# A decoder layer with a mixture of experts: the shared expert's products moved and stripped of their ones-products, b2 added as a row, the end divided among three engines

## The chip, the cores and the metric

The kernel runs on one core of a Trainium2 chip. Its engines work side by side, each through its own list of instructions in order: TensorE (PE in the profile, with PEld for its weight loads), VectorE (DVE), ScalarE (ACT), GpSimd (POOL) and SyncE (SP, which here only issues DMAs). ACT and POOL can issue DMAs too. Engines wait for one another by semaphores. The metric is the device time of one execution in microseconds (us); lower is better.

## The reference, cut to what matters

Two sequences of 1024 tokens with 256 features (N = 2048 tokens) go through self-attention, cross-attention over 77 context tokens, and a feed-forward block with 8 experts of which each token uses two. Each block sees a normalized input and is added to the running `x`. The change touches the end of cross-attention and the feed-forward block:

```python
probs = softmax(flat @ gate_W)                       # 2048 x 8
topk_w, topk_idx = top_k(probs, 2)
topk_w = topk_w / topk_w.sum(-1, keepdims=True)
combine = (one_hot(topk_idx, 8) * topk_w[..., None]).sum(1)
out = 0.5 * gelu(flat @ shared_W + shared_b)         # the shared expert
for e in range(8):
    h = gelu(flat @ W1[e] + b1[e])                   # 256 -> 1024
    out = out + combine[:, e:e+1] * (h @ W2[e] + b2[e])   # 1024 -> 256
out = layernorm(out, eps=1e-5) * gamma + beta
x = x + out
```

## The kernel before

All is float32. A *token tile* is 128 tokens (16 of them); a *chunk* c is four token tiles (4 chunks). `xs` holds x for all tokens, `xnT` the normalized input with features on the partitions, `acc` the feed-forward result of all tokens.

**Self-attention** takes the first 560 us and is not touched.

**Cross-attention and the sort.** One loop (before's lines 962 to 986) writes PE's order out by hand; the other engines' order is made by a scheduler from the same program. Per token tile i, `scores(i)` makes the products with the keys on PE, then DVE adds a mask and takes the maximum (L888), POOL subtracts it (L889), ACT takes the exponential (L892), DVE sums (L894) and inverts, POOL multiplies (L896); `turn(i)` transposes the result on PE into PSUM tiles named ppT, and ACT copies them. Per chunk, `queries(c)` prepares; `attend(c)` multiplies by the values in two halves (`pco`, L921, eight matmuls each, ACT copying each half into `oT`), then projects (`pu`, L933), and DVE adds the result to `xs` (L941); `gate(c)` normalizes `xs`, writes the rows to a DRAM table `xnd`, transposes them on PE into `xnT`, multiplies by the gate (`pg`, L953) and calls `choose(c)`: some 17 small DVE operations that find each token's two experts, `taken`, and the running count `earlier` (L764).

The sort turns this into a list of rows for each expert. `place(c)` multiplies `taken` and `earlier` by triangular and full matrices of ones on PE (`prk`, L772 and L776), then DVE computes each pair's slot and two one-hot tiles `row` and `col` (L802), and ACT multiplies `row` by the pair's number (L810). `invert(c)` multiplies `col` and `row` on PE (`pin`, L820) and DVE adds it into `places`. After chunk 3 the counts `pcn` give the tiles' owners; `ppk` (L1045), a product of `places`, gives `to_row` and `from_row` (L1053).

`shared(c)` is the shared expert: for each of the chunk's four token tiles a product of a row of ones with the bias row `fsb` (L833, the ones-product), and two products of `xnT` with `fsw` (L837), summed in PSUM; ACT takes Gelu of 128x1024 values into `acc` (L844). In PE's order shared(0) stands after place(2), shared(1) before place(3), shared(2) between place(3) and invert(3), and shared(3) after the sort, before the experts. POOL adds `beta_f` to `xs` with `add_rows` (L190), chunk by chunk, where the scheduler puts it.

**Experts.** The sorted pairs fill tiles of 256 rows, each with one expert: at least 16 (FULL), at most 23, and 19 in this run's data. For tile i, `fetch(i)`, issued two tiles ahead, loads the owner's W1 and W2 (1 MB each, SP's queue, three buffers each) and gathers the tile's rows `xg` by two indirect DMAs on POOL's queue (three buffers). `first_layer(i)` transposes `xg` on PE (`px`, L1134), DVE copies it to `xgT`, PE makes the products `ph` (L1144), ACT takes Gelu with b1 into `hT` (L1151). `second_layer(i)` multiplies by W2 (`po`, L1161), DVE copies the result to `y` (L1168), and two indirect DMAs on POOL's queue scatter it to a DRAM table `pairs` (L1171). PE's order is first_layer(0), first_layer(1), second_layer(0), first_layer(2), second_layer(1), and so on, with the transposes drawn a little ahead.

**End.** `weigh` made the two weights of each token and `comb`, tokens by experts. `biases(c)` transposes `comb`, multiplies by `b2` on PE (`pb2`, L1100), and DVE writes acc = 0.5 acc + pb2 (L1101). Then for each chunk two loads `yt` from `pairs` (SP's queue, four buffers), eight DVE operations that add weight x `yt` to `acc` (L1225), and `affine_residual`: DVE statistics (L149, L150), the power -0.5 on POOL (L142), and eight DVE operations (L197, L201) that normalize, scale by `gamma_f` and add `xs`; the chunk is stored from SP's queue.

Of the kernel before, what the change touches and what calls it, by code (L numbers as in the profile page):

```python
# [8 lines left out]
F32 = mybir.dt.float32  # L9
# [5 lines left out]
P = 128  # L15
# [23 lines left out]
def decoder_kernel(  # L39
# [73 lines left out]
    def load_bcast(src, name):  # L113
        t = const.tile([P, D], F32, name=name)
        nc.sync.dma_start(out=t, in_=src.rearrange("(o d) -> o d", o=1).to_broadcast([P, D]))
        return t
# [572 lines left out]
    fsb = rt.tile([1, D], F32, name="fsb")  # L689
    nc.sync.dma_start(out=fsb, in_=f_sb.rearrange("(o d) -> o d", o=1))  # L690
    b1 = rt.tile([E, HID], F32, name="b1")
    nc.scalar.dma_start(out=b1, in_=f_b1)
    b2 = rt.tile([E, D], F32, name="b2")
    nc.scalar.dma_start(out=b2, in_=f_b2)
# [133 lines left out]
    def shared(c):  # L828

        psh = big("psh").rearrange("p a (t f) -> p (a t) f", f=D)  # L830
        for t in range(4):
            tt = 4 * c + t
            nc.tensor.matmul(  # L833
                psh[:, t, :], lhsT=ones[0:1, :], rhs=fsb, start=True, stop=False
            )
            for kc in range(2):
                nc.tensor.matmul(  # L837
                    psh[:, t, :],
                    lhsT=xnT[:, kc, tt * P : (tt + 1) * P],
                    rhs=fsw[:, kc, :],  # L840
                    start=False,
                    stop=(kc == 1),
                )
        nc.scalar.activation(acc[:, 4 * c : 4 * c + 4, :], psh, AF.Gelu)  # L844

    with tc.tile_pool(name="cr1", bufs=1) as cr1, tc.tile_pool(name="cr2", bufs=2) as cr2:
# [65 lines left out]
        def attend(c):  # L912
            b = c // 2
            PT = PTs.pop(c)
            oT = cr2.tile([P, 2, 512], F32, tag="oT", name=f"oT{c}")
            for G in range(2):
                po = one("pco")
                for i in range(2):
                    for r in range(4):
                        h = 8 * G + 2 * r + i  # L920
                        nc.tensor.matmul(  # L921
                            po[32 * r : 32 * r + 32, :],
                            lhsT=vx[:T2, b, h, :, :].rearrange("p i d -> p (i d)"),
                            rhs=PT[:T2, h, :],
                            start=(i == 0),
                            stop=(i == 1),
                        )
                nc.scalar.copy(oT[:, G, :], po)
            for u in range(2):
                pu = one("pu").rearrange("p (t f) -> p t f", f=D)  # L930
                for t in range(2):
                    for G in range(2):
                        nc.tensor.matmul(  # L933
                            pu[:, t, :],
                            lhsT=oT[:, G, P * (2 * u + t) : P * (2 * u + t) + P],
                            rhs=cwu[:, G, :],
                            start=(G == 0),
                            stop=(G == 1),
                        )
                x2 = xs[:, 4 * c + 2 * u : 4 * c + 2 * u + 2, :]  # L940
                nc.vector.tensor_tensor(x2, x2, pu, ALU.add)  # L941
# [20 lines left out]
        with tc.manual_schedule(engines={nc.tensor.engine}):  # L962
            queries(0)
            for i in range(NT + 7):
                if i < NT:
                    scores(i)
                if 0 <= i - 2 < NT:
                    turn(i - 2)
                if i % 4 == 1 and i + 3 < NT:
                    queries(i // 4 + 1)  # L970
                if i % 4 == 3 and i > 3:
                    attend(i // 4 - 1)
                if i % 4 == 2 and i > 6:
# [12 lines left out]
            invert(3)  # L986
# [8 lines left out]
    with tc.tile_pool(name="ff1", bufs=1) as ff1, ExitStack() as later:  # L995
# [75 lines left out]
        shared(3)  # L1071
# [3 lines left out]
        comb = ff1.tile([P, NT, E], F32, name="comb")  # L1075

        def weigh():
# [6 lines left out]
            sel = ff1.tile([P, 2, NT, E], F32, name="selw")  # L1084
            nc.vector.tensor_tensor(
                sel, hots, wts.unsqueeze(3).to_broadcast([P, 2, NT, E]), ALU.mult
            )
            nc.vector.tensor_tensor(comb, sel[:, 0], sel[:, 1], ALU.add)

        def biases(c):  # L1090

            a4 = acc[:, 4 * c : 4 * c + 4, :]
            pct = one("pct").rearrange("p (t f) -> p t f", f=P)
            for t in range(4):
                nc.tensor.transpose(pct[:E, t, :], comb[:, 4 * c + t, :], ident)
            cT = ff1.tile([E, 4, P], F32, tag="cT", name="cT", bufs=2)
            nc.vector.tensor_copy(cT, pct[:E, :, :])  # L1097
            pb2 = big("pb2").rearrange("p a (t f) -> p (a t) f", f=D)
            for t in range(4):
                nc.tensor.matmul(pb2[:, t, :], lhsT=cT[:, t, :], rhs=b2, start=True, stop=True)  # L1100
            nc.vector.scalar_tensor_tensor(a4, a4, 0.5, pb2, ALU.mult, ALU.add)  # L1101
# [4 lines left out]
        hTs = [ff2.tile([P, NH, TS], F32, name=f"hT_{k}") for k in range(2)]  # L1106
        ys = [ff2.tile([P, 2, D], F32, name=f"y_{k}") for k in range(2)]

        def fetch(i):

            e = nc.sync.value_load(owner_i[0:1, i : i + 1], min_val=0, max_val=E - 1)
            w1, w2, xg = w1s[i % 3], w2s[i % 3], xgs[i % 3]
# [5 lines left out]
            )  # L1118
            for s in range(2):
                nc.gpsimd.indirect_dma_start(  # L1120
# [7 lines left out]
            return w1, w2, xg  # L1128

        def first_layer(i, w1, xg):  # L1130
# [8 lines left out]
            for q in range(2):  # L1139
                ph = big("ph").rearrange("p a (h f) -> p (a h) f", f=TS)  # L1140
                for j in range(4):
# [9 lines left out]
                    nc.scalar.activation(  # L1151
# [4 lines left out]
        def second_layer(i, w2, hT):  # L1156
# [11 lines left out]
            nc.vector.tensor_copy(y, po)  # L1168
# [44 lines left out]

        for c in range(4):
            biases(c)
        for c in range(4):
            a4 = acc[:, 4 * c : 4 * c + 4, :]
            for i in range(2):
                r0 = N * i + 512 * c
                yt = ff2.tile([P, 4, D], F32, tag="yt", name=f"yt_{c}{i}", bufs=4)  # L1220
                nc.sync.dma_start(
                    out=yt, in_=pairs[r0 : r0 + 512, :].rearrange("(t p) d -> p t d", p=P)
                )
                for t in range(4):
                    nc.vector.scalar_tensor_tensor(  # L1225
                        a4[:, t, :], yt[:, t, :], wts[:, i, 4 * c + t : 4 * c + t + 1],
                        a4[:, t, :], ALU.mult, ALU.add,
                    )
            affine_residual(a4, a4, c, gamma_f, 1e-5)
# [40 lines left out]
```

## Time and profile before

| What | Value |
|---|---|
| Time, three runs | 1150.11, 1150.76, 1152.16 us; median 1150.76 us |
| The profiled execution | 1148.25 us, span of its instructions 1146.4 us, mean granted PE clock 0.911 |
| Busy share of the span | PE 86%, PEld 49%, DVE 55%, ACT 44%, POOL 32% |
| choose(3) ended on DVE | 763.34 us |
| rows known (L1053) | 790.46 us |
| first transpose of the experts | 802.04 us |
| last matmul of the experts | 1087.7 us |
| first `yt` used | 1098.24 us |
| last DVE operation | 1140.95 us |
| weights (38 loads of 1024 KB, SP's queue) | median 8.7 us from issue to landing |
| gathers and scatters (38 each, POOL's queue) | median 6.2 and 3.0 us to landing |

How to read it: times within the kernel count from the span's start. A row of the timeline gives the start, the time that the group of instructions took, engine, line, operation, output <- inputs, shapes and count, and in brackets how long the engine sat idle before it and what ended that. A row of the waits gives who waited for whom: us in total, times, longest. A matmul of float32 appears as two passes. The granted clock is a share of PE's full clock.

### The profile page before, as it was taken

To read this page: it belongs to the slowest core of one execution; us is meant where nothing else is said; L and a number is where in the kernel's file an instruction comes from. 1 tells how busy PE (TensorE), PEld (TensorE's weight loads), DVE (VectorE), ACT (ScalarE), POOL (GpSimd) and SP (SyncE) were. 2 spreads that over 40 slices of the span, in tenths; PEclk is the share of its full clock that TensorE was granted. 3 is DMA by queue.
4 is the path that set the end of the run, shared out by engine and by line. 5 is a ranking of instruction groups with operands and counts; after the bars stand their busy time and mean duration, and the time that the engine had idled before them with its cause. 6 is when DMAs were issued, how large, how long until landed. Compare 5 with 4: busy or idle time off the path is not lost. (4 is left out here: it accounts for less than half of the span.)

```text
span 1146.4 us, 15580 instructions
## 1 busy us (share of the span) xinstructions
PE 984.9 (86%) x5926; PEld 563.2 (49%) x5926; DVE 627.1 (55%) x1208; ACT 502.3 (44%) x953; POOL 372.2 (32%) x308
## 2 busy tenths in 40 slices
PE   4889999999897999999367877899999999999940
PEld 2543333333332333332134555566888888887830
DVE  6776668778867788884785797442000000000167
ACT  1237667767664677779035343221322222222100
POOL 2123224443322333335576535113222222222101
PEclk9989999999898999999689887775999999999955
DMA  9100000000000000000000000005444445544042
GB/s 170 28 1 1 1 2 1 1 1 1 1 1 1 1 2 1 1 1 1 11 0 1 18 1 19 20 18 191 158 163 170 173 169 184 184 166 139 18 135 92
DMA packets 56741, 64.46 MB, mean 56 GB/s; under 512 B 17636, under 2 KB 49546, under 8 KB 56658
## 3 DMA queue, kind: packets, MB, share of 16 engines
q1 hardware_dynamic: 43634, 52.57, 13.6%
q0 software_dynamic: 3648, 9.18, 2.2%
q10 hardware_dynamic: 9376, 1.61, 1.0%
q8 instruction: 50, 0.82, 0.3%
q14 instruction: 33, 0.27, 0.1%
HBM read 54.97 MB, written 9.18 MB: 56 GB/s over the span
## 5 line engine op out<-in xcount | busy, mean ns | idle before, releaser
L516 DVE TENSOR_REDUCE mx<-sA 128x1 f32<-128x512 f32 x512 | 317.6, 683 | 87.6 <-PE sB L552 75.6
L560 ACT ACTIVATE pt<-sB 128x512 f32<-128x512 f32 x512 | 266.3, 611 | 113.7 <-PE sB L552 113.0
L509 PE MATMUL sA<-kT,qc 32*128 32x512 f32 x1024 | 264.6, 631 | 0.0
L552 PE MATMUL sB<-qB,kT 32*128 32x512 f32 x1024 | 253.0, 625 | 10.4 <-DVE mx L516 10.4
L582 POOL TENSOR_TENSOR avs<-avs,part 128x512 f32<-128x512 f32 x112 | 142.9, 1276 | 307.1 <-ACT part L581 306.7
L1151 ACT ACTIVATE hT<-ph,b1s 128x256 f32<-128x256 f32 x152 | 72.0, 474 | 200.0 <-PE ph L1144 200.0
L1168 DVE COPY y<-po 128x512 f32<-128x512 f32 x19 | 13.1, 692 | 259.8 <-PE po L1161 259.8
L509 PEld LDWEIGHTS sA<-kT,qc 32*128 32x128 f32 x1024 | 102.5, 187 | 91.2 <-ACT pt L560 56.1
L1161 PE MATMUL po<-w,hT 128*128 128x256 f32 x608 | 138.8, 382 | 5.6 <-DVE y L1168 5.6
L569 PE MATMUL av<-pt,vaug 128*32 128x512 f32 x1024 | 141.1, 612 | 0.9 <-ACT pt L560 0.9
L1144 PE MATMUL ph<-xgT,w 128*128 128x256 f32 x608 | 137.0, 384 | 0.5 <-DVE xgT L1138 0.5
L1161 PEld LDWEIGHTS po<-w,hT 128*128 128x128 f32 x608 | 114.1, 190 | 24.2 <-DVE y L1168 9.4
L552 PEld LDWEIGHTS sB<-qB,kT 32*128 32x128 f32 x1024 | 100.4, 187 | 51.0 <-issue 32.0
L1144 PEld LDWEIGHTS ph<-xgT,w 128*128 128x128 f32 x608 | 107.2, 190 | 27.4 <-ACT hT L1151 8.2
L1120 POOL DMA_INDIRECT xg<-xnd,from_row x38 | 37.1, 976 | 132.5 <-PE px L1134 88.9
L1171 POOL DMA_INDIRECT pairs<-y,to_row x38 | 38.3, 1007 | 125.9 <-DMA pairs<-y,to_row 76.2
L581 ACT COPY part<-av 128x512 f32<-128x512 f32 x112 | 69.0, 616 | 8.7 <-PE av L569 8.6
L569 PEld LDWEIGHTS av<-pt,vaug 128*32 128x32 f32 x1024 | 21.6, 109 | 101.3 <-DVE mx L516 84.2
L142 POOL TENSOR_TENSOR rstd<-rstd,nhalf 128x4 f32<-128x4 f32 x20 | 21.5, 1076 | 114.4 <-DVE rstd L141 114.0
L889 POOL TENSOR_TENSOR st<-st,cm 128x1232 f32<-128x1232 f32 x16 | 37.2, 2324 | 41.7 <-DVE cs L895 17.0
L908 ACT COPY PT<-ppT 77x1024 f32<-77x1024 f32 x32 | 30.8, 1005 | 43.7 <-PE ppT L907 43.7
L907 PE MATMUL ppT<-ident,st 128*77 128x128 f32 x256 | 37.5, 307 | 12.5 <-POOL st L896 6.8
(201 smaller groups left out, 998.9 us busy)
## 6 DMA issues: line engine op xcount, KB each, us to landing
w<-in_L_ffn_W_dram SPq DMA_DIRECT2D x38, 1024.0 KB, 8.7
yt<-pairs SPq DMA_DIRECT2D x8, 512.0 KB, 3.8
xs<-in_x_dram SPq DMA_DIRECT2D x4, 512.0 KB, 7.0
xnd<-xn SPq DMA_DIRECT2D x4, 512.0 KB, 2.9
out_dram<-acc SPq DMA_DIRECT2D x4, 512.0 KB, 3.0
mk<-in_mask_BxSxS_ik_dram SPq DMA_DIRECT2D x1, 616.0 KB, 4.6
xg<-xnd,from_row POOLq DMA_INDIRECT x38, 6.2
pairs<-y,to_row POOLq DMA_INDIRECT x38, 3.0
```

What stands on the lines that cost most here:

```text
L509: nc.tensor.matmul(s, lhsT=units[h // 4, "q"][r0 : r0 + 32, q0 : q0 + P], rhs=units[h // 4, "k", g % 2][r0 : r0 + 32, 512 * kh : 512 * kh ...
L516: nc.vector.tensor_reduce(largest[h][:, qt, hh : hh + 1, kh], s, AX.X, ALU.max)
L552: nc.tensor.matmul(s, lhsT=units[h // 4, "k", g % 2][r0 : r0 + 32, kt * P : (kt + 1) * P], rhs=shifted[h][r0 : r0 + 32, :], start=True, st ...
L560: nc.scalar.activation(powers[m, hh], s, AF.Exp, scale=1.0 / 16.0)
L569: nc.tensor.matmul(av[32 * hh : 32 * hh + 32, :], lhsT=vaug[:, kt, 4 * g + hh, :, b], rhs=powers.pop((m, hh)), start=True, stop=True,)
L581: nc.scalar.copy(part, av)
L582: nc.gpsimd.tensor_tensor(sums[h], sums[h], part, ALU.add)
L907: nc.tensor.transpose(pp[:T2, h, :], st[:, 8 * G + h, :], ident)
L1144: nc.tensor.matmul(ph[:, j, :], lhsT=w1[:, kc, hc * P : (hc + 1) * P], rhs=xgT[:, kc, :], start=(kc == 0), stop=(kc == 1),)
L1151: nc.scalar.activation(hT[:, hc, :], ph[:, j, :], AF.Gelu, bias=b1s[:, i, hc : hc + 1])
L1161: nc.tensor.matmul(po[:, s, :], lhsT=hT[:, hc, s * P : (s + 1) * P], rhs=w2[:, hc, :], start=(hc == 0), stop=(hc == NH - 1),)
L1171: nc.gpsimd.indirect_dma_start(out=pairs[:, :], out_offset=bass.IndirectOffsetOnAxis(ap=to_row[:, k : k + 1], axis=0), in_=y[:, s, :], in_ ...
```

## The change

- `shared(c)` has no ones-product any more; its two products per token tile start and stop the sum alone, and ACT copies the sum to `acc` without Gelu. `fsb` is loaded as a tile with the row on all partitions; POOL adds it to `acc` (128x1024, one operation a chunk), and after `hidden[1]` (the last Gelu of tile 1's hidden layer) `finish_shared(c)` takes Gelu of `acc` on ACT and halves it on DVE.
- PE's order around the sort: shared(0) stands between turn(14) and turn(15); place(c) stands between the two halves of attend(c+1); then attend(3) with place(2), shared(1), invert(2), gate(3), shared(2), place(3), pcn, shared(3), invert(3).
- POOL's `beta_f` additions, `fsb` additions and `weigh` are held behind the gathers of tiles 0 and 1. On POOL's list they now stand in this order: four gathers, the power of `weigh`, four fsb additions, four beta additions, then tile 2's gathers.
- `biases`, `comb` and b2's matmuls are gone. `fetch` loads the owner's b2 as a row on all 128 partitions (128 KB, SP's queue after W2, three buffers), and `y` is po + b2 on DVE instead of a copy.
- At the end the eight `yt` loads go into the weights' buffers, issued together from SP's and ACT's queues. Chunks 0 to 2: DVE adds the pairs and makes the statistics, ACT scales and shifts (four operations of 128x256), POOL multiplies by `gamma_f` and adds `xs` (two operations of 128x1024). Chunk 3 keeps `affine_residual` on DVE.

```diff
     def shared(c):
         psh = big("psh").rearrange("p a (t f) -> p (a t) f", f=D)
         for t in range(4):
             tt = 4 * c + t
-            nc.tensor.matmul(
-                psh[:, t, :], lhsT=ones[0:1, :], rhs=fsb, start=True, stop=False
-            )
             for kc in range(2):
                 nc.tensor.matmul(
                     psh[:, t, :],
                     lhsT=xnT[:, kc, tt * P : (tt + 1) * P],
                     rhs=fsw[:, kc, :],
-                    start=False,
+                    start=(kc == 0),
                     stop=(kc == 1),
                 )
-        nc.scalar.activation(acc[:, 4 * c : 4 * c + 4, :], psh, AF.Gelu)
+        nc.scalar.copy(acc[:, 4 * c : 4 * c + 4, :], psh)
...
                 nc.scalar.copy(oT[:, G, :], po)
+                if G == 0 and halfway is not None:
+                    halfway()
...
             queries(0)
-            for i in range(NT + 7):
+            for i in range(NT + 3):
...
                 if i % 4 == 3 and i > 3:
-                    attend(i // 4 - 1)
+                    attend(i // 4 - 1, (lambda c=i // 4 - 2: place(c)) if i > 7 else None)
+                if i == NT:
+                    shared(0)
                 if i % 4 == 2 and i > 6:
                     gate(i // 4 - 2)
-                if i % 4 == 3 and i > 10:
-                    place(i // 4 - 2)
-                if i == NT + 3:
-                    shared(0)
                 if i % 4 == 1 and i > 12:
                     invert(i // 4 - 3)
+            attend(3, halfway=lambda: place(2))
             shared(1)
+            invert(2)
+            gate(3)
+            shared(2)
             place(3)
             pcn = one("pcn")
             nc.tensor.matmul(pcn[:, :E], lhsT=ones, rhs=earlier[:, NT, :], start=True, stop=True)
-            shared(2)
+            shared(3)
             invert(3)
...
-        shared(3)
         sorting.__exit__(None, None, None)
...
-        def biases(c):
+        def finish_shared(c):
             a4 = acc[:, 4 * c : 4 * c + 4, :]
...
+            nc.scalar.activation(a4, a4, AF.Gelu)
+            nc.vector.tensor_scalar(a4, a4, 0.5, None, ALU.mult)
...
+            nc.sync.dma_start(out=b2, in_=f_b2[bass.ds(e, 1)].to_broadcast([P, D]))
             for s in range(2):
-                nc.gpsimd.indirect_dma_start(
+                fetched[i] = nc.gpsimd.indirect_dma_start(
...
-            nc.vector.tensor_copy(y, po)
+            nc.vector.tensor_tensor(y, po, b2.unsqueeze(1).to_broadcast([P, 2, D]), ALU.add)
...
         got = {0: fetch(0), 1: fetch(1)}
-        with tc.issue_after(sorted_at.ins):
+        with tc.issue_after(sorted_at.ins), tc.issue_after(fetched[1].ins):
             weigh()
-        for c in range(4):
-            add_rows(c, beta_f)
-        behind = tiles((0, FULL), FULL + 2, got, None)
+            for c in range(4):
+                a4 = acc[:, 4 * c : 4 * c + 4, :]
+                nc.gpsimd.tensor_tensor(
+                    a4, a4, fsb.unsqueeze(1).to_broadcast([P, 4, D]), ALU.add
+                )
+            for c in range(4):
+                add_rows(c, beta_f)
+        behind = tiles((0, 2), FULL + 2, got, None)
+        with tc.issue_after(hidden[1].ins):
+            for c in range(4):
+                finish_shared(c)
+        behind = tiles((2, FULL), FULL + 2, got, behind)
...
+        land = [w.rearrange("p a f -> p (a f)") for w in w1s + w2s]
+        yts = {}
         for c in range(4):
-            biases(c)
+            for i in range(2):
+                yt = land[c][:, 4 * D * i : 4 * D * (i + 1)].rearrange("p (t d) -> p t d", d=D)
+                r0 = N * i + 512 * c
+                (nc.sync, nc.scalar)[i].dma_start(
+                    out=yt, in_=pairs[r0 : r0 + 512, :].rearrange("(t p) d -> p t d", p=P)
+                )
+                yts[c, i] = yt
...
-            affine_residual(a4, a4, c, gamma_f, 1e-5)
+            if c == 3:
+                affine_residual(a4, a4, c, gamma_f, 1e-5)
+            else:
+                mv = stats(a4, 4)
+                r = norm_scale(mv, 4, 1e-5)
+                off = small.tile([P, 4], F32, tag="off", name="off")
+                nc.vector.scalar_tensor_tensor(
+                    off, mv[:, :, 0], -1.0, r[:, :4], ALU.mult, ALU.mult
+                )
+                for t in range(4):
+                    nc.scalar.activation(
+                        a4[:, t, :], a4[:, t, :], AF.Identity,
+                        bias=off[:, t : t + 1], scale=r[:, t : t + 1],
+                    )
+                nc.gpsimd.tensor_tensor(
+                    a4, a4, gamma_f.unsqueeze(1).to_broadcast([P, 4, D]), ALU.mult
+                )
+                nc.gpsimd.tensor_tensor(a4, a4, xs[:, 4 * c : 4 * c + 4, :], ALU.add)
```

More of the change, by code (lines that the diff above doesn't have):

```diff
@@ L688, in decoder_kernel @@
     fsw = load_rows(f_sw, "fsw", D, rt)
-    fsb = rt.tile([1, D], F32, name="fsb")
-    nc.sync.dma_start(out=fsb, in_=f_sb.rearrange("(o d) -> o d", o=1))
+    fsb = load_bcast(f_sb, "fsb", rt)
     b1 = rt.tile([E, HID], F32, name="b1")
     nc.scalar.dma_start(out=b1, in_=f_b1)
-    b2 = rt.tile([E, D], F32, name="b2")
-    nc.scalar.dma_start(out=b2, in_=f_b2)
     def counted(name, pattern, base, mult, shape):
```

44 lines of the change are left out of this document (14 added, 30 removed).

## The prediction

> **What bounds the kernel now.** I read the page's slices first, then the waits between 650 and 805 us, the order of time there, the granted clock by stretch, and the end. Slices are 28.66 us; TensorE (PE) fills most, but from slice 24 its clock falls, and in the last two VectorE (DVE) works almost alone.
>
> ```profile
> PE   4889999999897999999367877899999999999940
> DVE  6776668778867788884785797442000000000167
> PEclk9989999999898999999689887775999999999955
> ```
>
> Around the sort (650 to 805 us) one chain decides: gate, choose, place, the ACT products, invert, gather. The waits of that window show it standing twice behind PE, although PE had nothing of the chain to do:
>
> ```profile
> DVE places L826 <- PE pin L820: 13.1, 3, 9.6
> DVE at L781 <- PE prk L776: 8.0, 1, 8.0
> ```
>
> In order of time: choose(3) ends on DVE at 763.34, place(3) starts at 771.35 because shared(1) stands ahead of its two matmuls on PE; its ACT products end at 777.0, but invert(3) starts at 784.10, behind shared(2); the rows are known at 790.46, but the first transpose of the experts starts at 802.04, behind shared(3).
>
> ```profile
> 762.57 0.77 DVE L764 TENSOR_TENSOR earlier<-earlier,taken 128x8 f32<-128x8 f32 x4
> 771.35 0.19 DVE L781 TENSOR_TENSOR at<-prk,lane 128x32 f32<-128x32 f32 x1 [8.01 <-PE prk L776]
> 774.56 2.44 ACT L810 ACTIVATE row<-row,pair_no 128x128 f32<-128x128 f32 x8 [2.88 <-DVE row L802]
> 784.10 2.53 PE L820 MATMUL pin<-row,col 128*128 128x128 f32 x16
> 802.04 1.92 PE L1134 MATMUL px<-ident,xg 128*128 128x128 f32 x8
> ```
>
> The clock by stretch (us, then busy of PE, PEld, DVE, ACT, POOL, clock, DMA share, GB/s) shows how slow those shared products are:
>
> ```profile
> 761.20:789.50 28.30, 27.92 (x83) 18.20 (x82) 7.93 (x38) 4.49 (x10) 0.00 (x0) 0.56 0.06 16
> 840.00:1087.00 247.00, 240.87 (x1122) 199.52 (x1121) 21.40 (x33) 60.62 (x128) 59.62 (x60) 1.00 0.43 153
> ```
>
> At the end DVE waits for b2's matmuls after the first loads have landed, then needs 8.57 us a chunk (L149 starts at 1109.73, 1118.34, 1126.90, 1135.46), to 1140.95:
>
> ```profile
> 1098.24 0.88 DVE L1225 SCALAR_TENSOR_TENSOR acc<-yt,wts,acc 128x256 f32<-128x256 f32 x2 [5.86 <-DMA yt<-pairs]
> 1108.20 1.22 DVE L1101 SCALAR_TENSOR_TENSOR acc<-acc,pb 128x1024 f32<-128x1024 f32 x1 [1.80 <-PE pb L1100]
> 1109.73 0.74 DVE L149 BATCH_NORM_STATS2 bnst<-acc 128x6 f32<-128x256 f32 x2
> ```
>
> Attention up to 560 us and the 14.95 us of each expert tile are left as they are.
>
> **1. place inside attend: a loss.** PE now stops between the halves of attend until choose has ended. attend(1)'s first half ends at 667.5 (665.70 + 3.68/2), choose(0) at 672.0: PE stands 4.5 us, and pu, scores(12) and turn(10) queue behind it. DVE does place before it adds pu: from 672.7 small operations 0.6, cs 1.43, POOL's multiplication 2.25, which keeps the one-hots out (part 6), the one-hots 2.36: pu goes into xs at 679.5 instead of 673.55, 6.0 late. The second time choose(1) ends at 715.66, the first half at 712.9; by the same steps pu is added at 724.0 instead of 719.68, 4.3 late. What takes some back: two of POOL's beta additions (652.76 and 701.88, 2.35 each) leave this stretch, and PE waits there anyway (4.44 at 685.12). I put logits(2) 3 us late, 737.8 instead of 734.76 (bounds 0 and 10.3, both holds whole).
>
> **2. From logits(2) to places.** choose 3.68 gives 741.4, place(2)'s matmuls 0.7, attend(3)'s second half 2.6 (1.8 at full clock, 3.5 at half as before), oT 0.7, pu 3.9 (2.8 to 5.0): 749.3. Without ones-products shared(c) keeps 16 of its 24 matmul passes (shared(2) took 12.7, 771.63 to 784.3): by its own row at full clock 1.13 x 4 = 4.5, by its row at half 2.08 x 4 = 8.3. With 4.5 and invert(2)'s 2.0 the transposes start at 755.8 (xn is ready before: 749.3 + 0.7 sum, 1.3 stats, 1.1 power, 1.6 scaling), 0.5 late: choose(3), 8.0 after them as before (755.30 to 763.34), ends at 763.9. shared(2) runs 760.1 (pg's end, 759.62 before) to 764.6, then place(3)'s matmuls: DVE starts at 765.4, not 771.35. ACT's products end 5.65 later (771.35 to 777.0 before), 771.1; shared(3), 765.8 to 770.3, lies under them; invert(3) 2.0, copy 0.4: places at 773.5 instead of 786.96, **-13.5**. With attend at full clock too it is -15.3, and without the 3 us of part 1 -18.3. With shared(2) and (3) at half (8.3 each, to 768.4 and 777.9, invert(3) 2.5) it is -6.1, with attend at half as well -4.1. I take full clock for shared: without the one-row products it has the form of the expert rows (128*128, 128x256), which run at 1.00.
> The row is PE busy 27.92 of 28.30 us at clock 0.56. The Trainium skill (TensorE: Matmul & The Clock Gate, Part 1) says that some 3.4 us of sustained work bring the full clock. By the rule the clock would have come back before too and would be full in any case, -15.3; by the row busy time alone does not bring it, and -6.1 stays possible.
>
> **3. First transpose.** Rows to px was 11.6 (790.46 to 802.04). Now PE is free, and the gather ends it: second piece issued 2.58 after the rows, 5.7 to landing (median there; 2.7 to 7.3): 8.3, gain 3.3. PE stood idle, so its clock stays low longer: before, 1.7 us of the first layer ran at half; I add 0.9. **-2.4** (-5.4 to +0.7).
>
> **4. POOL's queue: a loss.** The fsb and beta additions, 8 x 2.36 = 18.9 us, now stand between the power for the weights (done 9.0 after the rows) and tile 2's gather. Its second piece is issued 29.2 after the rows, PE wants it 2.58 + 1.84 + 14.87 + 0.9 + 6.9 = 27.1 after them, the landing time being in both: **+2.1** (0 to 6.7, by the spread of landings). Tile 3's gather follows 2.5 later, tile 4's after that, both needed over 10 us later.
>
> **5. At nothing.** Four Gelus from SBUF (1.02 each) fit ACT's 9.27 us of idle before tile 2's hT; uncovered 4.1, once. DVE's four halvings (at most 1.22 each) and y's addition of b2 in place of a copy (PSUM row L941 0.69, copy 0.69) lie under PE. One more DMA a tile on SP (0.4 us) moves w1 by about 1 us; it is issued at 826.42 and used after 857. b2's row (128 KB beside 2 MB, DMA share 0.43) is issued three tiles ahead. ACT's Gelu table load (1.28) moves ahead of the first hT, under PE with three PSUM buffers.
>
> **6. The end.** Without b2's matmuls stats can start 8 x 0.40 = 3.2 after 1098.24 instead of 11.5: 8.3 gained. Chunks 0 to 2 now go to ACT and to two POOL operations of 2.35. These keep out DVE operations with two SBUF inputs:
>
> ```profile
> 679.95 1.22 DVE L802 TENSOR_TENSOR row<-part,iota_p 128x1024 f32<-128x1024 f32 x1
> 680.00 3.27 POOL L889 TENSOR_TENSOR st<-st,cm 128x1232 f32<-128x1232 f32 x1 [3.98 <-DVE bnmv L150]
> 681.09 3.27 DVE L802 TENSOR_TENSOR col<-part,iota_p 128x1024 f32<-128x1024 f32 x1
> ```
>
> POOL waited for row, col for POOL; alone they take 2.25 and 1.22. While POOL's two run, DVE gets one operation between them; a chunk then takes 2.35 + 0.40 + 2.35 + 0.40 + 0.09 (rstd) + 0.10 + 1.1 (power) + 0.06 + 0.12 (off) + 5 x 0.40 = 8.97, ACT's 4 x 0.41 lying under the last 2.0. First POOL product 9.08 after 1098.24 (3.2 + 1.9 stats + 0.9 + 1.2 + 0.2 + 1.7), two periods 17.94, the last chunk 8.51 (two POOL operations, two L197 at 0.39, 0.09, power 1.26, four L201 at 0.42): 1133.8 instead of 1140.95, **-7.1**. Without exclusion (ACT's chain and DVE's order alone) 1130.6, -10.4; with one more POOL operation in the way each chunk about -4. The eight loads on two queues land 512 KB each; at the weights' 389 GB/s (789.5 to 802.2) 1.3 us apiece, ahead of their use.
> Left on DVE, with b2 gone, the four chunks would end 31.22 (1109.73 to 1140.95) after 1101.44: 1132.7, 1.1 earlier than my sum. So the gain here is b2's, and sharing gives some of it back.
>
> **Sum:** -13.5 - 2.4 + 2.1 - 7.1 = -20.9. The profiled execution took 1148.25 (span 1146.4), 2.5 below the median of the runs; taken off the median 1150.76 this is **1129.9 us**.
>
> **Rivals.**
> - A. *Half clock stays* (0.20). For: clock 0.50 for 40 us of busy PE. Against: with the experts it was back at 805.6, 3.6 us after their first transpose. -6.1 - 2.4 + 2.1 - 7.1 = -13.5: 1137.3.
> - B. *attend's holds are paid whole* (0.12): 7.3 more than my 3: -13.6, 1137.2. For: PE, DVE and POOL are all in order there. Against: POOL loses two additions.
> - C. *Slower: b2's row is late* (0.10). y(i) waits on DVE for it; behind it stand xgT and PE's next first layer. It shares SP's queue with 2 MB a tile (8.7 us to land); gamma_f, of the same form, took 3.7. Exposed in 17 tiles that is 62.9 - 20.9 = +42: 1192.8; it decides from 20.9/17 = 1.23 us a tile. Against: the row is issued some 45 us before its use.
> - D. *The moves cancel* (0.03): PE stops in attend for what it saves later; about 1150.
>
> **How the numbers follow.** Forecast 0.55. Extremes added up are -34.1 (-18.3 - 5.4 - 10.4) and +6.6 (-4.1 + 0.7 + 6.7 - 4 + 7.3), all at once unlikely; eight in ten I put at 1118 to 1143, which takes in A and B with 6 us to spare and 12 us below the forecast, as part 2's best case and the end's (-3.3) would give together with part 1 unpaid. About 0.2% is what a measurement tells from no change: faster 0.87, same 0.03, slower 0.10.
>
> **What would show it.** place(3) starting within 2 us of choose(3); PE clock near 1 in shared(2) and (3); invert(3) directly after ACT's products; px ended by the gather; POOL adding for 19 us before tile 2's gather and one PE stall of about 2 us; period of about 9 us at the end with DVE waiting for POOL. Wrong if tiles take more than 15 us, if PE's stops in attend move logits(2) by over 6 us, or if the end's period is under 8.

## The result, and the profile after

The changed kernel takes 1149.89 us in the median of 20 runs (1147.16 to 1152.49); the kernel before, beside it, 1150.98 (1148.06 to 1153.70). The ratio is 0.9988, with an interval of 0.9977 to 0.9998: a gain of a tenth of a per cent, where 1.8% was forecast.

The profiled execution of the changed kernel has a span of 1150.0 us (1151.82 with what lies around it), 3.6 *more* than the profile before. It comes to the first copy of logits at 666.09 instead of 661.11, in a stretch that the change leaves alone but for one addition of beta that POOL no longer makes there (652.76 before). Run 1 below has the same program up to there and comes to it at 661.25 (more on that at the end). So the two traces are set side by side by stages, each from its own start. Every number is a difference of two start times in the traces (in the last row, of a start and the end of the span), and the last column is what the prediction had:

| stage | before | after | difference | predicted |
|---|---|---|---|---|
| start to logits(0) | 661.11 | 666.09 | +4.98 | 0 |
| logits(0) to the rows (from_row) | 129.16 | 117.75 | -11.41 | -13.5 |
| rows to the first y | 35.58 | 52.56 | **+16.98** | -2.4 + 2.1 |
| first y to last y | 261.87 | 261.86 | 0.0 | 0 |
| last y to the end | 58.68 | 51.74 | -6.94 | -7.1 |

Two of the three gains are there. They are lost again in one place, between the rows and the first y. The slices of the changed kernel (busy share in tenths, then PE's granted clock):

```profile
PE   4889999999797999999367787892799999999910
DVE  6677558777876788884886688645310000000047
PEclk9889999999988999999689777776799999999965
```

In slice 28, where the experts begin, PE is busy 2 tenths only. The waits of the window from 650 to 835 us (who, for whom, us in total, times, longest) name the reason:

```profile
PE ph L1131 <- DVE xgT L1125: 16.7, 1, 16.7
...
PE prk L769 <- DVE taken L759: 6.8, 2, 3.6
...
DVE places L823 <- PE pin L817: 5.3, 3, 3.7
DVE at L778 <- PE prk L773: 4.9, 4, 3.2
```

The two waits of before (13.1 and 8.0 us) have shrunk to 5.3 and 4.9, as meant; place inside attend costs PE 6.8; and a wait of 16.7 us for xgT, of which the same window has only 0.3 us before, stands on top. In order of time around the sort:

```profile
770.38 0.77 DVE L761 TENSOR_TENSOR earlier<-earlier,taken 128x8 f32<-128x8 f32 x4
774.34 0.19 DVE L778 TENSOR_TENSOR at<-prk,lane 128x32 f32<-128x32 f32 x1 [3.19 <-PE prk L773]
777.37 2.45 ACT L807 ACTIVATE row<-row,pair_no 128x128 f32<-128x128 f32 x8 [2.38 <-DVE row L799]
778.62 2.02 PE L817 MATMUL pin<-row,col 128*128 128x128 f32 x16 [0.55 <-DVE col L799]
792.42 0.45 PE L1121 MATMUL px<-ident,xg 128*128 128x128 f32 x1 [9.10 <-DMA xg<-xnd,from_row]
```

place(3) starts 3.2 us after choose(3) instead of 8.0, invert(3) begins before the ACT products are finished instead of behind shared(2), and px is ended by the gather. The clock by stretch (same columns as before; the stretch is the sort's last part):

```profile
766.18:783.84 17.66, 16.22 (x80) 13.87 (x79) 9.72 (x47) 4.36 (x10) 0.00 (x0) 0.80 0.11 32
```

The clock is 0.80 instead of 0.56. Then the place where the gain goes, on VectorE, POOL and PE (three answers of the same order of time, 783 to 830 us, each in its own fence):

```profile
793.07 18.40 DVE L1076 TENSOR_SCALAR wts<-wts 128x16 f32<-128x16 f32 x1 [8.96 <-POOL wts L1075]
811.51 0.25 DVE L1077 RECIPROCAL wts<-wts 128x16 f32<-128x16 f32 x1
811.79 0.17 DVE L1078 TENSOR_TENSOR wts<-wts 128x16 f32<-128x16 f32 x1
811.89 0.68 DVE L1125 COPY xgT<-px 128x512 f32<-128x512 f32 x1
```

```profile
793.02 9.23 POOL L1187 TENSOR_TENSOR acc<-acc,fsb 128x1024 f32<-128x1024 f32 x4
802.22 9.22 POOL L190 TENSOR_TENSOR xs<-xs,beta_f 128x1024 f32<-128x1024 f32 x4
```

```profile
812.63 3.78 PE L1131 MATMUL ph<-xgT,w 128*128 128x256 f32 x8 [16.71 <-DVE xgT L1125]
```

L1076 adds 1 to 16 numbers a row. Before, the same operation took 0.17 us:

```profile
799.49 0.17 DVE L1081 TENSOR_SCALAR wts<-wts 128x16 f32<-128x16 f32 x1 [8.95 <-POOL wts L1080]
```

Now it takes 18.40, from the moment POOL begins the eight additions to 0.03 us after the last ends. Behind it on VectorE stand the reciprocal, the weights' product and xgT, and for xgT waits PE.

The end, for its part, is as predicted (order of time; POOL's two operations of chunk 0, and VectorE's first weighted row of chunk 2 waiting for the gap between them):

```profile
1118.79 2.34 POOL L1245 TENSOR_TENSOR acc<-acc,gamma_f 128x1024 f32<-128x1024 f32 x1 [2.39 <-ACT acc L1241]
...
1120.02 1.38 DVE L1227 SCALAR_TENSOR_TENSOR acc<-w,wts,acc 128x256 f32<-128x256 f32 x1
1121.20 2.40 POOL L1248 TENSOR_TENSOR acc<-acc,xs 128x1024 f32<-128x1024 f32 x1
```

POOL's product comes at 1118.79, 1127.61 and 1136.44: a period of 8.83, where 8.97 was worked out. A single row of 0.40 takes 1.38 there.

### The profile page after: what moved, and what is told of

Its sections match the earlier page's. It is cut to its first block, busy times and chain, and to the rows that moved or that the text cites. A ratio compares the mean times of both kernels' runs of the same rounds, so it can differ in the third digit from the quotient of the medians.

```text
span 1150.0 us, 15494 instructions
## 1 busy us (share of the span) xinstructions
PE 956.5 (83%) x5846; PEld 547.5 (48%) x5846; DVE 644.6 (56%) x1181; ACT 513.2 (45%) x969; POOL 395.9 (34%) x318
## 5 line engine op out<-in xcount | busy, mean ns | idle before, releaser
L1156 DVE TENSOR_TENSOR y<-po,b 128x512 f32<-128x512 f32 x19 | 13.1, 692 | 240.6 <-PE po L1149 240.6
```

## The experiments

Theory T: POOL's eight additions, which follow one another with no wait between them, keep VectorE's L1076 out for as long as they run, and PE's first layer stands behind it. Rivals: L1076 is long for a reason of its own; or something else holds xgT. Medians are given with the runs' number; the kernel before, beside them, had 1150.9 to 1151.6.

**1. A stop after four of the eight additions.**

```diff
+            seen = ff1.tile([P, 1], F32, name="seen")
+            stop = nc.gpsimd.tensor_copy(seen, wts[:, 1, 0:1])
+        with tc.issue_after(stop.ins):
             for c in range(4):
                 add_rows(c, beta_f)
...
```

The edit also keeps tile 2's gather behind the last addition, where it stood.

> The changed kernel with one POOL copy of a single weight (128x1, it waits for the last of VectorE's weight operations) between the four fsb additions and the four beta additions; nothing else is moved. Theory T (VectorE's w0 = w1+1, 18.40 us in the changed kernel, is kept out by POOL's additions as long as they follow one another without a wait, and PE's first layer stands behind it): the stop ends the run after four, so w0 takes 9.2 us instead of 18.4, xgT and the first ph come 9.2 earlier, and the time falls by about 9 to 1141. Rival R1 (w0 is long for a reason of its own, POOL only beside it): w0 stays at 18.4, and POOL's beta additions then start only behind it; the time stays at 1150 or rises, up to 1159 if tile 2's gather goes 9 us further back. Rival R2 (a VectorE operation is let in after one POOL operation, as my prediction had it, and something else kept it out here): no change, 1150.

1137.81 us (4 runs), ratio to before 0.9884 (0.9867 to 0.9902). On VectorE and on POOL:

```profile
788.19 9.21 DVE L1076 TENSOR_SCALAR wts<-wts 128x16 f32<-128x16 f32 x1 [8.95 <-POOL wts L1075]
```

```profile
797.96 0.19 POOL L1191 COPY seen<-wts 128x1 f32<-128x1 f32 x1 [0.60 <-DVE wts L1078]
```

9.21 where 9.2 was expected; rows to first y falls from 52.56 to 42.85. The rest of the median's 12 us does not lie in this stage: this profile also comes to logits(0) at 661.25, 4.8 sooner than the changed kernel's.

**2. The stop ahead of all eight.** The same copy, between the weights and the first addition of fsb; tile 2's gather stays behind the additions.

> The changed kernel with the same POOL copy of a single weight ahead of all eight additions. Theory T: w0 takes 0.2 us at 793, the eight additions run from about 794.5 to 813, and xgT, which reads PSUM, is copied at 796 beside them, if a copy out of PSUM is not kept out: first ph at 797 instead of 812.6. Tile 2's gather is issued 1.3 us later than now and lands at about 821, where PE wants it at 820.6: a stall of 0 to 3 us. Gain 12.5 to 15.5, time 1134.5 to 1137.5. If copies out of PSUM are kept out too (T2), xgT waits until 813 and nothing is gained: 1150 to 1151. Rival R1 (w0 long for a reason of its own): w0 long again, 1150 or more.

1133.89 us (4 runs), ratio 0.9847 (0.9830 to 0.9863). L1076 takes 0.17 us, rows to first y 35.41. That copies out of PSUM are not kept out is seen in the same stretch, POOL's additions first and xgT beside them:

```profile
790.96 9.27 POOL L1190 TENSOR_TENSOR acc<-acc,fsb 128x1024 f32<-128x1024 f32 x4
```

```profile
791.56 0.69 DVE L1125 COPY xgT<-px 128x512 f32<-128x512 f32 x1 [0.81 <-PE px L1121]
```

Tile 2's gather is issued at 809.64 and 811.00, after the additions, and PE's px(2) runs at 816.06 without a wait for it: the 2.1 us which the prediction charged for the late gather are zero. But y(1) comes 16.47 after y(0) instead of 14.95; PE waits 1.25 for ACT's hT there, for a reason that stays open (see 6).

**3. Tile 2's gather ahead of the additions.** No stop; the gather's two issues (2.3 us) lie between the power and the first addition.

```diff
         with tc.issue_after(sorted_at.ins), tc.issue_after(fetched[1].ins):
             weigh()
+        got[2] = fetch(2)
+        with tc.issue_after(fetched[2].ins):
             for c in range(4):
...
-                if i + 2 < last:
+                if i + 2 < last and i + 2 not in got:
```

> The changed kernel with tile 2's gather ahead of the eight additions on POOL and nothing added. The two issues of the gather (2.5 us) leave VectorE its weight operations. Theory T: w0 0.2 us, first ph at about 797, no stall at tile 2; gain 15.6, time 1134 (1132 to 1136), which is my prediction's sum with its +2.1 for the late gather taken away and attend's hold as it was measured. T2 (copies out of PSUM are kept out by the additions too): xgT of tile 0 waits until 814, no gain, 1150. The difference to the run with the stop ahead of the additions is what a late gather of tile 2 costs: predicted 2.1.

1130.26 us (5 runs), ratio 0.9822 (0.9805 to 0.9840). Rows to first y is 34.73, 0.9 less than before the change. One moved gather takes the median from 1149.89 to 1130.26, 19.6 us; everything else in the kernel is as it was. The two profiles differ by 21.8 us: 17.8 between the rows and the first y, 4.8 ahead of logits(0), where nothing was edited, and 1.1 lost again between y(0) and y(1). Runs 2 and 3 both came out below the times expected of them (1134.5 to 1137.5, and 1132 to 1136), which were worked out from the changed kernel's one profile.

**4. The end left on VectorE**, added to run 3 (`if c == 3:` becomes `if c >= 0:`).

> As the run with tile 2's gather first, and the end of all four chunks left on VectorE (the old form of norm and residual, without b2's matmuls), so that only the sharing among three engines is undone. My prediction's working: four chunks need 31.2 from the first statistics, 34.4 from the first landed pair, against 35.3 measured shared: 1 us earlier, 1133. Rival S (sharing pays: the old end's 8.57 a chunk had slack that the shared one hasn't): 2 to 4 us later than the shared end. Rival S2 (loads, not engines, set the end): no difference within 0.5.

1131.32 us (5 runs), ratio 0.9823 (0.9805 to 0.9841): not to be told from run 3 by the medians. By stages, last y to the end is 50.79 against 51.87: 1.08 less, where the prediction had 1.1. Run 9, which has this end too, has 51.17, 0.7 less.

**5. A gap of POOL's own.** Behind each fsb addition, a POOL copy of one element that it just made; it waits for no other engine.

```diff
...
+                with tc.issue_after(stop.ins if c else fetched[1].ins):
...
+                seen = ff1.tile([P, 1], F32, name=f"seen{c}")
+                stop = nc.gpsimd.tensor_copy(seen, acc[:, 4 * c + 3, D - 1 : D])
...
```

The beta additions stay behind the last copy, and tile 2's gather behind them.

> The changed kernel, its order kept, with a POOL copy of one element of the sum just made behind each of the four fsb additions: it waits for no other engine, only POOL itself has to finish an addition before it. My prediction's assumption was that VectorE gets one operation in between two of POOL's. Theory G (it does so wherever POOL's next operation needs the result of its last, as gamma's product and the residual's addition at the end do, and not where the additions are independent of each other): w0 takes about 2.4 us instead of 18.4, the reciprocal is let in at the next gap and w1's product at the one after, so xgT is copied at about 800.5 instead of 811.9 and the time falls by 11: about 1139. Rival W (only a stop that waits for another engine lets VectorE in, as in the two runs with a stop): w0 stays near 18 or takes the five gaps in one piece, 1150.

1135.66 us (4 runs), ratio 0.9866 (0.9849 to 0.9884). VectorE's three operations of the weights:

```profile
791.24 2.32 DVE L1076 TENSOR_SCALAR wts<-wts 128x16 f32<-128x16 f32 x1 [8.96 <-POOL wts L1075]
793.59 0.25 DVE L1077 RECIPROCAL wts<-wts 128x16 f32<-128x16 f32 x1
793.88 2.22 DVE L1078 TENSOR_TENSOR wts<-wts 128x16 f32<-128x16 f32 x1
```

So VectorE does get in between two POOL operations, and here it did where the second needs a result of the first. The copy differs from an addition in size and kind too, so that the needed result is the cause was not tried by itself; the changed kernel's end agrees with it, where POOL's second operation needs the first, both are 128x1024, and a row of VectorE's gets in between. Over the four kernels L1076 takes 18.40, 9.21, 2.32 and 0.17 us for eight, four, one and no additions in one piece: 2.3 each. The reciprocal ran beside POOL's small copy and needed no gap of its own, which is why the gain is 13.9 (rows to first y 38.65) and not 11.

**6. The four Gelus set apart**, one behind each first layer of tiles 1 to 4, added to run 3.

```diff
-        with tc.issue_after(hidden[1].ins):
-            for c in range(4):
+        for c in range(4):
+            with tc.issue_after(hidden[c + 1].ins):
                 finish_shared(c)
-        behind = tiles((2, FULL), FULL + 2, got, behind)
+            behind = tiles((c + 2, c + 3), FULL + 2, got, behind)
+        behind = tiles((6, FULL), FULL + 2, got, behind)
```

> As the run with tile 2's gather first (1130.3), with the four Gelus of the shared expert set apart, one behind the first layer of each of tiles 1 to 4 instead of all four behind tile 1's. There PE waited for ACT's hT three times in tile 2, and tile 1's y came 16.04 us after tile 0's instead of 14.95. Theory: one Gelu of 0.95 us fits ACT's pause of 8.4 us between two tiles with room to spare, as four of 3.9 should have; if the wait in tile 2 is the Gelus', 1.1 us is gained: 1129.2, at the edge of what five rounds can tell; the trace tells it by the step from y(0) to y(1). Rival (the wait comes from w1 or the gather of tile 2 and not from ACT): the step stays at 16.0.

1131.93 us (5 runs), ratio 0.9832 (0.9819 to 0.9845): no gain that runs can tell. In the trace, y(0) to y(1) is 14.95 again and first y to last y 261.85 instead of 262.96. That alone would make the 1.1 us the Gelus', but the other traces speak against it. With the four Gelus together at the same place, the step is 14.95 or 14.96 in the changed kernel and in runs 1 and 5, 15.1 to 15.2 in runs 4, 7 and 8, 16.04 in run 3 and 16.47 in run 2. With the Gelus set apart it is 14.95 or 14.96 in runs 6, 9 and 10, but 15.75 in run 11. And in run 3 the last of the four ends at 810.72, and ACT is idle for 5.49 us before tile 2's first hT; the late ones are the second and the third, which begin 0.93 and 0.97 us after the one ahead of them has ended, instead of 0.39. So it is not ACT being busy with the Gelus, and what holds hT there stays open.

**7. place behind attend**, added to run 3: `halfway()` is called after the second half's sums.

> As the run with tile 2's gather first (1130.3), with place taken out of attend again: it is issued behind the second half instead of between the halves. The changed kernel's trace has PE waiting 3.59 and 3.18 us for choose in the middle of attend(1) and attend(2), and logits(3) comes 2.8 us later than before once the later start of that run is taken off. Theory H (that is the price of place inside attend, as the prediction's part 1 had it with 3 us): 2.8 us gained, 1127.5. Rival (PE's stop is covered, since PE waits for scores' softmax there anyway, and the 2.8 come from the order behind it): no change, 1130. Rival (place(2) later delays the products and invert(2), which stands ahead of gate(3) on PE): a loss of up to 4, 1134.

1127.96 us (5 runs), ratio 0.9801 (0.9780 to 0.9823). By stages (logits(0) as the start): logits(2) 74.87 instead of 77.77, logits(3) 100.36 instead of 101.10, the rows 115.47 instead of 117.36. So the hold costs 2.9 at logits(2), as the prediction's 3 had it, but only 1.9 reach the rows. The kernel before has 98.55 at logits(3): the other 1.8 are not the hold's and were not looked into. Run 9, whose order is the same up to there, has 94.55, 5.6 us of it by the clock in attend(3) (see the end), so a comparison of two profiles at this point is no finer than that.

**8. One-row products back in the shared expert**, with a row of zeros, added to run 3.

```diff
+            nc.tensor.matmul(
+                psh[:, t, :], lhsT=ones[0:1, :], rhs=zrow, start=True, stop=False
+            )
```

> As the run with tile 2's gather first (1130.3), with a one-row product put back into each of the 16 products of the shared expert, by a row of zeros, so that the additions on POOL stay and the sum is the same. Theory K (the one-row products keep PE's clock at half, the prediction's reason to cost the shared products at full clock without them): shared(2) and shared(3) take about 12.5 us each instead of 6.7 and 3.7, place(3) starts 5.8 later, and invert(3) stands behind shared(3), so places come 10 to 12 us later: about 1141. Rival P (the clock follows something else, and the one-row products cost only their own passes, 4 x 0.28 us a chunk at full clock and twice that at half): places 2 to 3 us later, 1132 to 1133.

1161.24 us (6 runs, 1155.77 to 1161.53), ratio 1.0082 (1.0064 to 1.0099): slower than before the change. shared(2) and shared(3) take 12.68 us each, first start to last end. The clock from the start of the one to the end of the other, and one step of shared(3), a pair of one-row products and four of 128 rows:

```profile
777.14:803.31 26.17, 26.17 (x55) 15.24 (x55) 8.57 (x42) 3.46 (x9) 0.00 (x0) 0.50 0.00 1
```

```profile
790.83 1.22 PE L832 MATMUL psh<-zrow,ones 1*128 1x256 f32 x2
791.98 2.08 PE L836 MATMUL psh<-fsw,xnT 128*128 128x256 f32 x4
```

PE is busy all of 26.17 us at half clock. Without the one-row products the same 128-row products brought it to full speed inside shared(2): in run 3 it takes 6.54 us, and shared(3) 3.70. What this shows is that a low clock did not come back with the one-row products mixed in, not that they always lower it: shared(0) and shared(1) of this run find the clock at 1.00 and keep it, at 6.81 us each. In the kernel before, shared(1) also begins at 1.00 and falls to 0.50 some 2 us later, although PE is busy all the time (0.71 from 761 to 762, 0.50 from 762 on); what made the difference was not tried. The rows come 23.2 us later than in run 3, twice what was expected, because shared(0) and shared(1), which stand ahead of gate(3), also grew (6.6 at logits(3)) and invert(3) ran at half clock too. The rest of the median's 31 is in the stretch up to logits(0), 8.3 later than in run 3, of which some 5 are found between runs of one kernel; the other 3 stay open.

**9 to 11. Other ends**, on top of runs 6 and 7: all on VectorE; the residual alone on POOL (`nc.vector` for gamma's product); both on VectorE with ACT scaling.

> The run with place behind attend (1128.0), with the four Gelus set apart over tiles 1 to 4 and the end of all chunks on VectorE, b2 still a row. By the traces of those edits made singly: 0.85 for the end (34.5 from the first weighted row to the end instead of 35.3) and 0.3 to 1.1 for the Gelus: 1126 to 1127. Rival (the medians of single edits differ by the runs' spread and not by the edits): 1128 or above.

> As the run before it in this list, but chunks 0 to 2 of the end shared in another way: ACT scales the rows as in the changed kernel, VectorE multiplies by gamma (128x1024 out of two SBUF inputs, 1.22 as the one-hots of the same form) and POOL keeps only the addition of the residual, which then runs beside VectorE's statistics of the next chunk. Theory X (only VectorE's operations with two SBUF inputs, or in its fast form, wait for POOL; statistics, at 0.39 and 0.17 beside POOL in the changed kernel, don't): a chunk takes 8 x 0.41 + 2.3 statistics + 0.25 + 1.22 + some 0.4 of waiting = 7.5 instead of 8.83 shared or 8.56 on VectorE: 3 x 1.06 = 3.2 less than with the end on VectorE, 31.3 from the first weighted row to the end: 1123. Rival (a POOL operation always costs VectorE its own 2.35): period 9.4, 1129.

> As that run, with the residual's addition on VectorE too (1.22), so that POOL has no large operation at the end. Period 8 x 0.41 + 2.3 + 0.25 + 2 x 1.22 = 8.3, 3 x 0.26 = 0.8 less than all on VectorE: 1125.5. Theory X has this 2.4 slower than with the residual on POOL; its rival has it 3 faster.

1127.83 (5 runs), 1130.26 (5) and 1130.62 us (6 runs, 1121.36 to 1131.17), where 1126 to 1127, 1123 and 1125.5 were expected; ratios 0.9804 (0.9782 to 0.9827), 0.9811 (0.9790 to 0.9832) and 0.9808 (0.9779 to 0.9837). The medians can't rank them. By stages, last y to the end is 51.17, 50.16 and 50.03. The residual on POOL has a period of 8.21, not 7.5: the statistics do run beside POOL's addition at 0.39, but only about 1 us of them is left when it starts, and then a weighted row waits 1.65 for it. Theory X is right in what waits and was wrong in the order of work: it had run 10 2.4 us ahead of run 11, and by the stage it is 0.13 behind. Run 11's period, 8.13 with no large operation on POOL, says that the sharing is a draw.

**12. The end and b2's row alone**, on the kernel before.

> The kernel before with the part of the change that begins at the expert tiles and nothing of the rest: b2 as a row by DMA for each tile and added into y, halvings by VectorE behind xgT of tile 1, the eight loads on two queues, the end among three engines. The shared expert with its ones-products and Gelus, place, invert and the beta additions stand as before. My prediction's part 6 has 7.1 us for it, and the changed kernel's trace 6.9 from the last y to the end, with the steps between two tiles unchanged at 14.95: 1144 (before 1151), and the step between tiles at 14.95 here too. If the end's gain comes only together with the earlier parts (a late b2, the halvings in the way of xgT, the loads): less than 5, 1146 or more.

1144.21 us (6 runs), ratio 0.9944 (0.9926 to 0.9962): 7.0 less than the kernel before beside it (1151.21). First y to last y is 261.87, as before to the hundredth, so b2's row, its addition into y and one more DMA for each tile cost nothing; last y to the end is 52.08 instead of 58.68, 6.6 of the 7.0.

Of all runs, 7 and 9 are the fastest, at 1128, some 2% below both kernels; the forecast for the change as it stood was 1129.9, and the time came there only with one gather moved (run 3).

## Why the prediction was wrong

**Part 1, right in kind, 1.4 too little.** PE stopped 3.59 and 3.18 us in attend; logits(2) came 4.4 later than before instead of 3, inside the bounds of 0 and 10.3, and 2.9 of it is by run 7 the hold.

**Part 2, right in kind.** From logits(0) to the rows, -11.4 instead of -13.5. Of the 2.1 that are missing, 1.4 are part 1's. Logits(2) to logits(3) took 23.4 for the text's 22.4, logits(3) to places 13.5 for 13.3, and 0.4 came back between places and the rows. "I take full clock for shared" held for shared(0), shared(1) and shared(3) (3.62 to 3.70 us, less than the 4.5 of the text) and not for shared(2) (6.66), so place(3) started 3.2 us after choose(3) and not within 2; little of that reached places, and invert(3) began before ACT's products had ended. That the clock does not come back while one-row products are mixed in was argued in the prediction and is shown by run 8. The rule that the prediction weighed (the Trainium skill, TensorE: Matmul & The Clock Gate, Part 1: some 3.4 us of sustained work bring the full clock) fails on run 8's row, 26.17 us busy at 0.50, and comes nearer with products of 128 rows alone: in the changed kernel shared(2) stood at 0.50 from its start to 773, 5.7 us, and at 1.00 from 774.

**Part 3, right for px, too much for the first y.** Rows to px is 8.58 us instead of 11.77, -3.2, for the 3.3 of the text before it takes off 0.9 for the clock. But in run 3, where xgT no longer waits, the first y comes only 0.9 sooner after the rows than before (34.73 for 35.58), and 0.1 to 0.6 sooner in runs 2, 4 and 6 to 11, where the text had 2.4. PE waits again for the second piece of the rows (0.86 in run 3), and the first sixteen passes of `ph` take 6.3 us in run 2 and 5.6 in run 3 instead of 4.7. In run 2 that is a clock which stays low for longer than the 0.9 allowed; in run 3 it is 0.92 of waiting for the first hT, behind ACT's table load of 1.28. The upper bound of +0.7 does not follow from the part's own terms: with a landing of 7.3 they give -0.8.

**Part 4 is the step that failed.** The text says of the eight additions that they "now stand between the power for the weights (done 9.0 after the rows) and tile 2's gather", and charges **+2.1** for the gather alone. It followed POOL's own queue and not VectorE's. On VectorE, the weights' three operations behind the power stand ahead of xgT, and the first of them starts at the very moment POOL starts adding. The gather's delay cost 0 (run 2); keeping VectorE out cost 17 to 18 (rows to first y 52.56 in the changed kernel, 35.41 in run 2 and 34.73 in run 3). The text had half of the mechanism in its hands: part 6 reads from the profile that POOL's operations "keep out DVE operations with two SBUF inputs", and it was not applied to part 4. That rule covers the weights' product L1078, but not L1076, which has one such input. The profile before had a case of that form too, beside POOL's subtraction (2.25 us from 689.63), and it was not read:

```profile
690.46 1.44 DVE L141 TENSOR_SCALAR rstd<-bnmv 128x4 f32<-128x4 f32 x1
```

With no POOL operation beside it L141 takes 0.16. And had the rule been applied, its price would have been too small: "While POOL's two run, DVE gets one operation between them" is true of two operations of which the second needs the first (run 5, and the end), and false of eight independent ones: 2.3 by that sentence, 18.40 measured. The Trainium skill (SBUF — State Buffer, section SBUF: two separate sides) says of the pair of SBUF ports which VectorE and GpSimd share that it is locked for a whole instruction and the other engine blocks until then. The traces agree that VectorE waits, and differ on how long: for independent POOL operations it was the whole row of them, 9.21 for four and 18.40 for eight.

**Part 5, right** for b2's row, y's addition and the extra DMA (run 12: 261.87 from first y to last y, as before). For the four Gelus no cost is shown (run 6); the table load cost 0.92 in run 3. **Part 6, right**: -6.9 for -7.1, period 8.83 for 8.97, and -6.6 with nothing else of the change (run 12); sharing loses 0.7 to 1.1 to VectorE alone (runs 9 and 4), for 1.1.

**The rivals.** A (half clock stays) happened to part of shared(2); its ground, "clock 0.50 for 40 us of busy PE", passes over 786 to 788, where the clock before stood at 1.00 behind invert(3)'s products of 128 rows. B and C did not. D named the time, 1150, and not the cause: what cancels the gain is not PE in attend but VectorE at the first expert. No case of the prediction had a transposed tile waiting behind the weights. With that one cost taken away, run 3 is at 1130.26; its stages sum to -18.4 against the -20.9 forecast, so the closeness of the median to 1129.9 is 2.5 us of luck.

## What to carry to other kernels

Work moved to POOL has two queues to be checked: POOL's, and VectorE's over the time POOL will be busy; look there for any operation with two SBUF inputs, or an fp32 scalar operation from SBUF to SBUF, and for who waits behind it. A row of independent POOL operations counted as one long operation here. A short wait (run 1) or a POOL operation that needs the last one's result (run 5) opened it, and two DMA issues ahead of it (run 3) let VectorE's work through first, which was worth 17.8 us of the stage. Compare traces by stages that start at the same event, since the whole span moves by 5 us and more from one execution to the next.

## What the runs showed of the hardware, not expected

Besides the row of additions: what is kept out and what isn't. Beside POOL's large operations, an fp32 scalar operation from SBUF on 16 elements a row waited (18.40), as did operations with two SBUF inputs (1.38, 1.65, 2.22), while a copy out of PSUM (0.69) and statistics (0.39 and 0.40) did not.

And PE's clock can differ within one and the same order of instructions. Runs 9 and 10 issue the same on PE up to the end; attend(3)'s two products, first of run 9, then of run 10:

```profile
737.82 3.64 PE L915 MATMUL pco<-PT,vx 77*32 77x512 f32 x32
741.39 4.06 PE L927 MATMUL pu<-cwu,oT 128*128 128x256 f32 x16
```

```profile
740.48 7.06 PE L915 MATMUL pco<-PT,vx 77*32 77x512 f32 x32
747.47 6.20 PE L927 MATMUL pu<-cwu,oT 128*128 128x256 f32 x16
```

That is 5.6 us, and the rows come 110.67 after logits(0) instead of 115.45. Of all fourteen profiles, the kernel before included, run 9's is the only one with `pco` of attend(3) at full clock. A second such difference lies at the start: the mean clock of the first 100 us is 0.97 in the profile before and 0.91 in the profile after, and POOL's first addition of attention's beta comes at 197.4 and 202.0: 4.6 of the 5 us up to logits(0) are lost by then. What decides either was not tried.
